# Counting edges with stretches of 6 end nodes and 256 edges in place of 8 and 384, in a graph network kernel on one core

## The chip, the cores and the metric

The kernel runs on one core of a Trainium2 chip. The metric is the device time of one execution in microseconds. A core has a matrix engine (TensorE, PE in the rows; PEld is its loading of weights), a vector engine (DVE), an activation engine (ACT), GpSimd (POOL) and a queue for transfers (SP). They run side by side and wait for each other by semaphores. [...]

## The reference

A graph has 2500 nodes with 256 features and 80000 edges, sorted by their end node `dst`. Three layers of an edge convolution follow a layer norm, and a last product takes the concatenation of all four node states.

```python
def _edge_conv(x, src, dst, W, b):
    xi = x[dst]
    xj = x[src]
    m = jnp.concatenate([xi, xj - xi], axis=-1) @ W + b
    s = jax.ops.segment_sum(m, dst, num_segments=N)
    cnt = jax.ops.segment_sum(jnp.ones((dst.shape[0],), m.dtype), dst, num_segments=N)
    return s / jnp.maximum(cnt, 1.0)[:, None]
...
for W, b in ((W0, b0), (W1, b1), (W2, b2)):
    h = jax.nn.relu(_edge_conv(h, src, dst, W, b))
    xs.append(h)
cat = jnp.concatenate(xs, axis=-1)
return cat @ Wf + bf          # h starts as max(layernorm(x), 0); x is added to this result
```

Since the sum over edges is linear, a layer needs only the matrix A of counts, A[s, d] being the number of edges from s to d. With Wt and Wb the two halves of W, the new state of node d is the ReLU of h[d] (Wt - Wb) + (sum over s of A[s, d] (h Wb)[s]) / count[d] + b.

## The kernel before

**Counting.** End nodes are cut into stretches of `W` = 8 consecutive nodes, `NW` = 313 of them. As edges are sorted by end node, the edges of a stretch lie in one run; for each stretch `CAP` = `CH` * 128 = 384 edges are taken from the run's start on, more than any stretch has. An edge has two keys: `key_m` is its start node within a tile of 128 nodes, `key_n` is (tile of the start node) * 8 + (end node within the stretch), and far outside for edges that are not of the stretch. `build(g, a)` makes the columns of A for a group of 384 end nodes. In each step it takes `BW` = 3 stretches and has DVE compare the keys with `iota_m` and `iota_n` (line 505): this gives 0/1 masks `one_m` (128 edges x 128 start nodes for each of 9 chunks of edges) and `one_n` (128 edges x 160 cells, `NB` = 20 tiles * 8). PE multiplies them (line 513), one product for each chunk, three accumulating for a stretch, and ACT copies 3 x 160 = 480 columns of counts from the PSUM bank into `a` (line 515). The masks lie in two buffers each (pool `hot`), so DVE can be two steps ahead of PE. A group has 16 such steps; `GT` = 3 tiles of 128 nodes make a group and 7 groups cover all nodes, the last with 200 columns.

**Preparation.** Where each stretch's run starts is found on the chip: `WG` blocks of 128 stretches (3 before) each gather one row of 625 end nodes (line 382, POOL), cast it (line 386, ACT) and count the entries below the stretch's first node (line 388, DVE). Then each block gathers its end and start nodes (line 404), forms the keys (lines 408 to 420), transposes them on PE (line 424) and stores them (line 426, ACT). `W` passes of DVE (line 430) count the edges of each end node. If the sum of these counts isn't the number of edges, another function (`general`) computes everything again.

**Layers.** `nodes_split` computes h Wb and splits it into two parts `zh`, `zl`. `layer(l, g)` runs `final` (line 525, the last product's share), `own` (line 541, h (Wt - Wb)) and 80 products of `zh` and `zl` with the counts (line 558). In layer 0 the counts of group g+1 are built while layer 0 runs on group g: `weave` interleaves the two in the program's text by a fixed ratio, 16 steps of `build` against 25 of `layer`. Each group of counts is also written to memory (line 520) and read back in layers 1 and 2 (line 607). A scheduler places the instructions of each engine in an order of its own from this text.

Of the kernel before, what the change touches and what calls it, by code (L numbers as in the profile page):

```python
# [9 lines left out]
I32 = mybir.dt.int32  # L10
# [259 lines left out]
def by_windows(ctx: ExitStack, tc: tile.TileContext, x, src, dst, Ws, bs, Wf, bf, out, missing):  # L270
    nc = tc.nc
    P = 128
    N, D = x.shape
    E = src.shape[0]
    NT = (N + P - 1) // P
    NP = NT * P
# [1 line left out]
    L = len(Ws)  # L278
    DC = D // P
    R = E // P  # L280
    W = 8
    CH = 3
    CAP = CH * P
    NW = (N + W - 1) // W
    NV = NW * W
    WG = (NW + P - 1) // P
    NB = NT * W
    BW = 3
    GT = 3
    G = GT * P  # L290
    GW = G // W
    NG = (NV + G - 1) // G
    FAR = 1024.0
    assert NP * FAR < 2 ** 24
    assert E == P * R and N % 2 == 0 and NV <= NP and BW * NB <= 512 and CAP < 4096 and NB <= 256
    assert E + P < 2 ** 24 and GW % BW == 0

    const = ctx.enter_context(tc.tile_pool(name="const", bufs=1))
# [6 lines left out]
    def bank():  # L305
        return ps.tile([P, 512], F32, name="bank")
# [5 lines left out]
    zl = const.tile([P, NT, D], F32R, name="zl")  # L312
    key_m = const.tile([P, NW, CH, 4], BF16, name="key_m")
    key_n = const.tile([P, NW, CH, 4], BF16, name="key_n")
    share = const.tile([P, NV], F32, name="share")
# [4 lines left out]
    iota_n = const.tile([P, NB], BF16, name="iota_n")  # L320
    b_sb = const.tile([P, L, DC], F32, name="b_sb")
    bf_sb = const.tile([P, D], F32, name="bf_sb")
    a_dram = [dram.tile([P, NT, G], F32, name=f"a_dram{g}") for g in range(NG)]
    deg_dram = dram.tile([2, WG * P * W], F32, name="deg_dram")


    pre = ctx.enter_context(ExitStack())
    pp = pre.enter_context(tc.tile_pool(name="pre", bufs=1))
# [26 lines left out]
    lim_i = pp.tile([P, WG], I32, name="lim_i")  # L355
    nc.gpsimd.iota(lim_i, pattern=[[P * W, WG]], base=0, channel_multiplier=W)
    lim = pp.tile([P, WG], F32, name="lim")
    nc.vector.tensor_copy(lim, lim_i)
    im_i = pp.tile([P, NB], I32, name="im_i")
    nc.gpsimd.iota(im_i, pattern=[[1, NB]], base=0, channel_multiplier=0)  # L360
    nc.vector.tensor_copy(iota_m, im_i[:, :P])
    nc.vector.tensor_copy(iota_n, im_i)

    first = pp.tile([P, 1], F32, name="first")
    nc.vector.tensor_copy(first, first_i)
# [11 lines left out]
    base = pp.tile([P, WG], F32, name="base")  # L377
# [21 lines left out]
    for i in range(WG):  # L399
# [21 lines left out]
        for keys, k in ((key_m, km), (key_n, kn)):  # L421
            pt = bank()
            for j in range(CH):
                nc.tensor.transpose(pt[:, j * P:(j + 1) * P], k[:, j * P:(j + 1) * P], ident)  # L424
            for j in range(CH):
                nc.scalar.copy(keys[:, i * P:i * P + n, j, :],
# [66 lines left out]
    def group_of(g):  # L493
        return g * G, min(G, NV - g * G)

    def build(g, a):
        w0, n = g * GW, group_of(g)[1] // W
        for s in range(0, n, BW):
            nb = min(BW, n - s)
            ws_ = slice(w0 + s, w0 + s + nb)  # L500
            one_m = hot.tile([P, BW * CH, P], BF16, name="one_m")
            one_n = hot.tile([P, BW * CH, NB], BF16, name="one_n")
            for one, iota, keys, m in ((one_m, iota_m, key_m, P), (one_n, iota_n, key_n, NB)):
# [110 lines left out]
def gnn_kernel(tc: tile.TileContext, x, src, dst, Ws, bs, Wf, bf, out):  # L614
    nc = tc.nc
    with tc.tile_pool(name="flag", bufs=1) as flag:
        missing = flag.tile([1, 1], I32, name="missing")
        by_windows(tc, x, src, dst, Ws, bs, Wf, bf, out, missing)
        again = nc.values_load(missing, min_val=0, max_val=1)
        with tc.If(again > 0):  # L620
            general(tc, x, src, dst, Ws, bs, Wf, bf, out)
# [28 lines left out]
```

## Time and profile before

| | |
|---|---|
| time of three runs | 614.01, 615.08 and 619.92 us, median 615.08 us |
| the profiled execution | 615.26 us, of which 613.5 us are its span from the first instruction to the last |
| busy in the span | PE 546.9, PEld 485.9, DVE 303.3, ACT 134.5, POOL 25.2 us |
[...]

A busy time counts the stretches in which an engine had at least one instruction under way. Products on PE overlap in the rows, since one begins before the one ahead has drained; the distance between two starts tells what one costs in a row of them, not its duration. In time the program has four parts: preparation to 48.5 us; `nodes_split` of layer 0 and the start of counting to 88 us; the counts of group 0 alone to 112 us; layer 0 interleaved with counting to 279 us. Then nothing is counted any more.

### The profile page before, as it was taken

The page shows a single profiled execution, that of the slowest core. Times are in us where ns is not written, and L with a number is a line of the kernel's source. Part 1 is how long each engine was busy: PE and PEld are TensorE (multiplying, and loading weights), DVE is VectorE, ACT ScalarE, POOL GpSimd, SP SyncE. Part 2 cuts the span into 40 slices and gives each one's busy share as a digit, 9 for nine tenths or more (in the row PEclk, how much of TensorE's full clock was granted, in tenths as well). Part 3 has the DMA queues.
Part 4 walks back from the last instruction along what each step waited for, and adds up shares of the span by engine and source line. Part 5 has one row for each costly group of instructions (what it writes and reads, how often), then busy time and mean ns, then how long its engine had stood idle before and what let it go on. Part 6 is the DMA issues. An engine that isn't in the chain of part 4 may idle for free.

```text
span 613.5 us, 8181 instructions
## 1 busy us (share of the span) xinstructions
PE 546.9 (89%) x3409; PEld 485.9 (79%) x3409; DVE 303.3 (49%) x617; ACT 134.5 (22%) x274; POOL 25.2 (4%) x37
## 2 busy tenths in 40 slices
PE   0036767999999999999999999999999999999996
PEld 0014555798989898989889999999988999999995
DVE  4694239989898989892240222202251220122233
ACT  0354643423333333331130000000031000000000
POOL 0422320000000000000000000000000000000000
PEclk9999997999999999999999999999999999999999
DMA  9314000606060605056920664344660533664013
GB/s 277 96 45 169 1 18 2 257 1 257 2 257 1 258 2 256 2 256 199 388 98 0 257 256 179 141 194 135 263 268 1 210 144 161 257 256 135 2 61 111
DMA packets 21277, 90.13 MB, mean 147 GB/s; under 512 B 2824, under 2 KB 18192, under 8 KB 18672
## 3 DMA queue, kind: packets, MB, share of 16 engines
q1 hardware_dynamic: 14272, 82.14, 34.1%
q10 hardware_dynamic: 6336, 5.26, 2.7%
q0 software_dynamic: 624, 2.14, 1.3%
q8 instruction: 28, 0.46, 0.3%
q14 instruction: 17, 0.14, 0.1%
HBM read 61.30 MB, written 28.23 MB: 146 GB/s over the span
## 4 chain that ended last, share of the span: by engine, by line
PE 83%; DVE 6%; DMA 4%; issue 3%; ACT 2%; POOL 1%; SPq 0%; DVEq 0%; POOLq 0%
PE pa L558 45%; PE bank L525 11%; PE bank L513 9%; PE bank L473 9%; PE bank L541 8%; DVE junk L430 2%; DMA wt<-in_L_gnn_W_dram 2%; DMA wb<-in_L_gnn_W_dram 1%; DVE one_n L505 1%; DVE one_m L505 1%; ACT zh L475 1%; ACT hT L485 1%; DMA es<-in_src_dram,start_i 1%; POOL rows L382 0%; DVE kn L418 0%
## 5 line engine op out<-in xcount | busy, mean ns | idle before, releaser
L558 PE MATMUL pa<-a,zh 128*128 128x384 f32 (+1 forms) x840 | 280.4, 341 | 0.7 <-ACT a L515 0.7
L558 PE MATMUL pa<-a,zl 128*128 128x384 f32 (+1 forms) x840 | 270.8, 329 | 0.0
L558 PEld LDWEIGHTS pa<-a,zh 128*128 128x128 f32 x840 | 158.4, 189 | 3.1 <-issue 0.9
L558 PEld LDWEIGHTS pa<-a,zl 128*128 128x128 f32 x840 | 158.5, 189 | 2.3
L563 DVE TENSOR_TENSOR v<-pa,share 128x384 f32<-128x384 f32 (+1 forms) x42 | 20.2, 523 | 213.0 <-PE pa L558 213.0
L505 DVE TENSOR_TENSOR one_n<-iota_n,key_n 128x1440 bf16<-128x1440 bf16 (+1 forms) x105 | 93.9, 895 | 0.0
L513 PE MATMUL bank<-one_n,one_m 128*128 128x160 bf16 x939 | 86.8, 240 | 6.5 <-DVE one_n L505 6.2
L513 PEld LDWEIGHTS <-one_m 128*128 128x128 bf16 x939 | 67.0, 101 | 25.4 <-issue 12.4
L505 DVE TENSOR_TENSOR one_m<-iota_m,key_m 128x1152 bf16<-128x1152 bf16 (+1 forms) x105 | 78.6, 749 | 11.8 <-PE bank L513 11.8
L515 ACT CAST a<-bank 128x480 fp32r<-128x480 f32 (+1 forms) x105 | 58.5, 558 | 110.4 <-PE bank L513 110.2
L543 ACT ACTIVATE u<-bank,b_sb 128x384 f32<-128x384 f32 (+1 forms) x42 | 23.5, 560 | 241.8 <-DVE acc L527 156.4
L525 PE MATMUL bank<-wf,hT 128*128 128x256 f32 x320 | 74.1, 381 | 0.0
L473 PE MATMUL bank<-wb,hT 128*128 128x256 f32 x240 | 60.0, 397 | 11.1 <-ACT hT L485 10.2
L525 PEld LDWEIGHTS bank<-wf,hT 128*128 128x128 f32 x320 | 59.5, 190 | 6.9
L473 PEld LDWEIGHTS bank<-wb,hT 128*128 128x128 f32 x240 | 44.7, 194 | 21.9 <-ACT hT L485 15.3
L541 PE MATMUL bank<-hT,wt 128*128 128x384 f32 (+1 forms) x168 | 55.2, 466 | 0.0
L476 DVE TENSOR_TENSOR zl<-bank,zh 128x256 fp32r<-128x256 f32 x60 | 25.2, 423 | 46.0 <-ACT zh L475 45.9
L541 PEld LDWEIGHTS bank<-hT,wt 128*128 128x128 f32 x168 | 30.7, 190 | 14.3
L475 ACT CAST zh<-bank 128x256 fp32r<-128x256 f32 x60 | 22.4, 373 | 61.1 <-PE bank L473 61.1
L527 DVE TENSOR_TENSOR acc<-acc,bank 128x256 f32<-128x256 f32 x80 | 30.4, 414 | 9.7 <-PE bank L525 9.7
L424 PE MATMUL bank<-ident,km 128*128 128x128 f32 x9 | 2.7, 439 | 33.1 <-ACT km L420 33.1
L424 PEld LDWEIGHTS bank<-ident,km 128*128 128x128 f32 x9 | 1.5, 212 | 34.2 <-ACT km L420 34.2
(66 smaller groups left out, 161.6 us busy)
## 6 DMA issues: line engine op xcount, KB each, us to landing
a<-a_dram SPq DMA_DIRECT2D x12, 3840.0 KB, 12.0
a_dram<-a SPq DMA_DIRECT2D x6, 3840.0 KB, 10.8
a<-a_dram SPq DMA_DIRECT2D x2, 2000.0 KB, 9.8
out_dram<-acc ACTq DMA_DIRECT2D x19, 128.0 KB, 1.7
a_dram<-a SPq DMA_DIRECT2D x1, 2000.0 KB
acc<-in_x_dram ACTq DMA_DIRECT2D x3, 640.0 KB, 8.0
some<-deg_dram SPq DMA_DIRECT2D x1, 1252.0 KB, 6.3
share<-deg_dram SPq DMA_DIRECT2D x1, 1252.0 KB
```

The costliest lines, as they stand in the source:

```text
L473: nc.tensor.matmul(pz[:, :D], hT[:, c, t * P:(t + 1) * P], ws[l][1][:, c, :], start=(c == 0), stop=(c == DC - 1))
L475: nc.scalar.copy(zh[:, t, :], pz[:, :D])
L476: nc.vector.tensor_sub(zl[:, t, :], pz[:, :D], zh[:, t, :].bitcast(F32))
L505: nc.vector.tensor_tensor(one[:, :k, :].rearrange("p k (m r) -> p k m r", r=4), iota.rearrange("p (m r) -> p m r", r=4).unsqueeze(1).to_br ...
L513: nc.tensor.matmul(pb[:, w * NB:(w + 1) * NB], one_m[:, w * CH + j, :], one_n[:, w * CH + j, :], start=(j == 0), stop=(j == CH - 1))
L515: nc.scalar.copy(a[:, :, s * W:(s + nb) * W].rearrange("p t (w c) -> p t w c", c=W), pb[:, :nb * NB].rearrange("p (w t c) -> p t w c", w=n ...
L525: nc.tensor.matmul(po[:, :D], hT[:, c, t * P:(t + 1) * P], wfs[l][:, c, :], start=(c == 0), stop=(c == DC - 1))
L527: nc.vector.tensor_add(acc[:, t, :], acc[:, t, :], po[:, :D])
L541: nc.tensor.matmul(pw_[:, :n], ws[l][0][:, c, o * P:(o + 1) * P], hT[:, c, c0:c0 + n], start=(c == 0), stop=(c == DC - 1))
L543: nc.scalar.activation(u[:, o, :n], pw_[:, :n], AF.Identity, bias=b_sb[:, l, o:o + 1])
L558: nc.tensor.matmul(pa[:, o, :n], z[:, k, o * P:(o + 1) * P], a[:, k, :n], start=(k == 0 and z is zh), stop=(k == NT - 1 and z is zl))
L563: nc.vector.tensor_mul(v[:, :n], pa[:, o, :n], share[:, c0:c0 + n])
```

## The change

Stretches have 6 end nodes (`W` = 6) and 256 edges (`CH` = 2), and a step of `build` takes `BW` = 4 of them. There are 417 stretches in place of 313, and `WG` is 4 in place of 3. The tile's place in `key_n` still counts in steps of 8 (`S`), so `iota_n` holds 20 x 6 = 120 of the values 0 to 159. A step has 8 products of 120 columns in place of 9 of 160; its masks are 8 x 128 and 8 x 120 elements on each partition in place of 9 x 128 and 9 x 160; ACT still copies 480 columns. A full group still has 16 steps. The last group has 198 columns in place of 200, and its build 33 stretches in place of 25, in 9 steps as before.

```diff
-    W = 8
-    CH = 3
+    W = 6
+    CH = 2
+    S = 8
     CAP = CH * P
     NW = (N + W - 1) // W
     NV = NW * W
     WG = (NW + P - 1) // P
     NB = NT * W
-    BW = 3
+    BW = 4
...
-    im_i = pp.tile([P, NB], I32, name="im_i")
-    nc.gpsimd.iota(im_i, pattern=[[1, NB]], base=0, channel_multiplier=0)
+    im_i = pp.tile([P, NT * S], I32, name="im_i")
+    nc.gpsimd.iota(im_i, pattern=[[1, NT * S]], base=0, channel_multiplier=0)
     nc.vector.tensor_copy(iota_m, im_i[:, :P])
-    nc.vector.tensor_copy(iota_n, im_i)
+    nc.vector.tensor_copy(iota_n.rearrange("p (t c) -> p t c", c=W),
+                          im_i.rearrange("p (t c) -> p t c", c=S)[:, :, :W])
```

In the interleaved part the order on PE stays the same but for the count of products in a burst and, twice in a group, one product of line 558 that changes sides of a burst. The order moves in the preparation. On ACT, at the casts of the gathered rows (`rows_f`), where the first two normalised tiles (`h0`) stand too; before:

```order
L461 ACTIVATE rs_385<-rs_385 128x20
L386 CAST rows_f_156<-rows_154 128x625
L480 ACTIVATE h0_398<-acc_76,off_389,rs_385 128x256
L480 ACTIVATE h0_410<-acc_76,off_389,rs_385 128x256
L420 CAST km_180<-lo_i_171 128x384
L426 CAST key_m_80<-bank_182 128x128x4 x3
L426 CAST key_n_81<-bank_189 128x128x4 x3
```

and now:

```order
L463 ACTIVATE rs_408<-rs_408 128x20
L388 CAST rows_f_158<-rows_156 128x625
L482 ACTIVATE h0_421<-acc_76,off_412,rs_408 128x256
L482 ACTIVATE h0_433<-acc_76,off_412,rs_408 128x256
L388 CAST rows_f_164<-rows_162 128x625
L422 CAST km_188<-lo_i_179 128x256
L428 CAST key_m_80<-bank_190 128x128x4 x2
L428 CAST key_n_81<-bank_195 128x128x4 x2
```

The cast of the fourth block's row stands behind the two `h0`. On POOL, at the gathers of the rows and of the edges (`ed`, `es`); before:

```order
L382 DMA rows_142<-in_dst_dram,blk_i_138 128x625
L382 DMA rows_148<-in_dst_dram,blk_i_138 128x625
L382 DMA rows_154<-in_dst_dram,blk_i_138 128x625
L404 DMA ed_166<-in_dst_dram,start_i_141 128x384
L404 DMA es_165<-in_src_dram,start_i_141 128x384
```

and now:

```order
L384 DMA rows_144<-in_dst_dram,blk_i_140 128x625
L384 DMA rows_150<-in_dst_dram,blk_i_140 128x625
L384 DMA rows_156<-in_dst_dram,blk_i_140 128x625
L384 DMA rows_162<-in_dst_dram,blk_i_140 128x625
L483 TENSOR_TENSOR acc_76<-acc_76,bf_sb_89 128x256 x2
L406 DMA ed_174<-in_dst_dram,start_i_143 128x256
L406 DMA es_173<-in_src_dram,start_i_143 128x256
```

Besides the fourth gather, two additions to `acc`, which stood behind all gathers, now stand ahead of those of the edges.

## Rows read from the trace of the kernel before

**Rows 1.** Page, chain that ended last: share of the span by line.
```profile
PE pa L558 45%; PE bank L525 11%; PE bank L513 9%; PE bank L473 9%; PE bank L541 8%; DVE junk L430 2%; DMA wt<-in_L_gnn_W_dram 2%; DMA wb<-in_L_gnn_W_dram 1%; DVE one_n L505 1%; DVE one_m L505 1%; ACT zh L475 1%; ACT hT L485 1%; DMA es<-in_src_dram,start_i 1%; POOL rows L382 0%; DVE kn L418 0%
```

**Rows 2.** Busy time by stage: stretch, length, engines' busy us, granted clock, transfers.
```profile
0.00:48.50 48.50, 6.15 (x21) 3.54 (x22) 34.30 (x141) 15.40 (x29) 11.65 (x19) 1.00 0.45 132
88.60:112.96 24.36, 17.19 (x153) 13.62 (x151) 24.07 (x33) 9.15 (x17) 0.00 (x0) 0.79 0.10 32
142.75:172.80 30.05, 30.05 (x245) 26.17 (x245) 28.08 (x42) 10.14 (x18) 0.00 (x0) 1.00 0.31 132
```

**Rows 3.** Groups of instructions, PE, one group of the interleaved part (142.75 to 172.80).
```profile
L513 PE MATMUL bank<-one_n,one_m 128*128 128x160 bf16 x144 | 12.7, 234 | 0.0
```

**Rows 4.** Timeline: products (PE), then weight loads (PEld), around one burst's end; start, duration.
```profile
151.66 0.44 PE L513 MATMUL bank<-one_n,one_m 128*128 128x160 bf16 x4
151.89 0.42 PE L558 MATMUL pa<-a,zh 128*128 128x384 f32 x1
152.15 0.33 PE L558 MATMUL pa<-a,zl 128*128 128x384 f32 x1
152.32 0.34 PE L558 MATMUL pa<-a,zh 128*128 128x384 f32 x1
...
151.30 0.18 PEld L513 LDWEIGHTS <-one_m 128*128 128x128 bf16 x3 [0.18 <-DVE one_n L505]
...
151.87 0.19 PEld L558 LDWEIGHTS pa<-a,zh 128*128 128x128 f32 x1
151.98 0.19 PEld L558 LDWEIGHTS pa<-a,zl 128*128 128x128 f32 x1
```

**Rows 5.** Timeline, PE: two of the 80 products of the last group, 200 columns.
```profile
292.05 0.28 PE L558 MATMUL pa<-a,zl 128*128 128x200 f32 x1
292.16 0.27 PE L558 MATMUL pa<-a,zh 128*128 128x200 f32 x1
```

**Rows 6.** Groups by shape, DVE, whole span: the masks at two widths, the counting passes.
```profile
L505 DVE TENSOR_TENSOR one_n<-iota_n,key_n 128x1440 bf16<-128x1440 bf16 x104 | 93.5, 899 | 0.0
L505 DVE TENSOR_TENSOR one_m<-iota_m,key_m 128x1152 bf16<-128x1152 bf16 x104 | 78.3, 753 | 11.8 <-PE bank L513 11.8
L430 DVE TENSOR_SCALAR_CACHE_REDUCE junk<-away 128x384 bf16<-128x384 f32 x16 | 7.9, 538 | 0.0
...
L371 DVE TENSOR_SCALAR_CACHE_REDUCE junk<-bank,lim 128x128 f32<-128x128 f32 x3 | 0.9, 343 | 0.0
...
L505 DVE TENSOR_TENSOR one_n<-iota_n,key_n 128x480 bf16<-128x480 bf16 x1 | 0.4, 400 | 0.0
L505 DVE TENSOR_TENSOR one_m<-iota_m,key_m 128x384 bf16<-128x384 bf16 x1 | 0.3, 349 | 0.0
```

**Rows 7.** Timeline, DVE: masks of group 0's third step and of the first step after it.
```profile
89.23 0.75 DVE L505 TENSOR_TENSOR one_m<-iota_m,key_m 128x1152 bf16<-128x1152 bf16 x1
...
110.28 0.75 DVE L505 TENSOR_TENSOR one_m<-iota_m,key_m 128x1152 bf16<-128x1152 bf16 x1
```

**Rows 8.** Timeline of the preparation: ACT, DVE and POOL, starts of the blocks.
```profile
23.69 0.70 ACT L386 CAST rows_f<-rows 128x625 f32<-128x625 int32 x1
24.42 0.87 DVE L388 TENSOR_SCALAR_CACHE_REDUCE junk<-rows_f,lim 128x625 bf16<-128x625 f32 x1 [0.33 <-ACT rows_f L386]
25.42 1.09 ACT L480 ACTIVATE h<-acc,off,rs 128x256 f32<-128x256 f32 x2 [1.03 <-DVE off L464]
29.12 0.47 DVE L408 TENSOR_SCALAR away<-ed,lim 128x384 f32<-128x384 int32 x1 [3.42 <-DMA ed<-in_dst_dram,start_i]
33.73 1.41 POOL L481 TENSOR_TENSOR acc<-acc,bf_sb 128x256 f32<-128x256 f32 x2
35.64 0.41 DVE L408 TENSOR_SCALAR away<-ed,lim 128x384 f32<-128x384 int32 x1
47.36 0.74 DVE L505 TENSOR_TENSOR one_m<-iota_m,key_m 128x1152 bf16<-128x1152 bf16 x1
```

**Rows 9.** Busy time by stage, as in rows 2: a stretch within group 0's counting.
```profile
102.48:109.31 6.83, 5.90 (x39) 4.63 (x40) 6.83 (x10) 2.45 (x5) 0.00 (x0) 0.51 0.00 0
```

More of the change, by code (lines that the diff above doesn't have):

```diff
@@ L293, in by_windows @@
     FAR = 1024.0
-    assert NP * FAR < 2 ** 24
-    assert E == P * R and N % 2 == 0 and NV <= NP and BW * NB <= 512 and CAP < 4096 and NB <= 256
+    assert NP * FAR < 2 ** 24 and W <= S and NT * S <= 256
+    assert E == P * R and N % 2 == 0 and NV <= NP and BW * NB <= 512 and CAP < 4096
     assert E + P < 2 ** 24 and GW % BW == 0
```

## The prediction

> **What bounds the kernel now.** I read the chain that ended last first, then the busy times by stage, then single rows. In the chain the reader is to see that PE carries it, with 9% of the span in the products that count edges, line 513 [rows 1]. The stages tell where those lie on the path [rows 2]. In the interleaved part PE is busy all of its 30.05 us in each group, while DVE has 28.08 and ACT 10.14: PE is the bound there, with DVE close behind. While group 0 is counted alone (88.60 to 112.96) it is the other way round: DVE is busy 24.07 of 24.36 us and PE 17.19. In the preparation DVE has the most, 34.30 of 48.50 us, but in a chain with gathers. From 279 us on nothing is counted, so more than half of the time has no part in it: layers 1 and 2 and the last product are the same but for a last group of 198 columns instead of 200.
>
> **The products in the interleaved part.** Four products of a burst take 0.44 us from the first start to the last end [rows 4], and one lasts 0.234 us [rows 3], so starts stand (0.44 - 0.234)/3 = 0.069 us apart. [...] For 120 columns I take 50 + 2.5 = 52.5 ns.
>
> What ends a burst matters too. The product of line 558 behind it starts its weight load at 151.87, when the last narrow product starts; the second such load follows 0.11 us later, at 151.98, and the second product begins at 152.15, 0.26 us behind the first, where 0.17 is usual (from there to the next start, 152.32) [rows 4]. The wide load of 0.11 us thus covers the last narrow product, whether that takes 69 or 52 ns. So a burst counts by its gaps: eight of 69.2 ns before, 554 ns, seven of 52.5 now, 368 ns, and 186 ns are saved. Five groups are built fully in this part with 16 bursts each, the last group's build has 8 full bursts and one of two products instead of three: 88 x 0.186 + 0.09 = **16.5 us saved**. If the last product counted fully it would be 88 x 0.203, 1.5 us more.
>
> Does the weight load let a product be that short? It is loaded anew for each product, 128 columns. Three bf16 loads are through in 0.18 us, the drain of the last counted in [rows 4]: at most 0.06 us each. With that bound as the pace, 88 x 7 x 7.5 ns = 4.6 us of the gain are lost. I take none, because the end of the third load is drain that would overlap, and keep 4.6 for the range. [...]
>
> [...]
>
> DVE must keep up. Its masks have a slope: one_m (753 - 349)/768 = 0.526 ns per element, one_n (899 - 400)/960 = 0.520 [rows 6]. A step has 128 and 480 elements fewer: 67 + 250 = 317 ns less. DVE's 28.08 us of a group become 28.08 - 16 x 0.317 = 23.0, against PE's 30.05 - 16 x 0.186 = 27.1. PE stays the bound, with more room than before. ACT copies 480 columns in 16 steps as before, with runs of 6 cells in place of 8; its 10.14 of 30 us hide even a doubling.
>
> **Group 0 alone.** Two steps are masked ahead; the third starts at 89.23 and the seventeenth, the first of group 1, at 110.28: 14 steps of 1.504 us, DVE without a gap [rows 7]. They lose 14 x 0.317 = 4.4 us. The last burst behind them is 0.2 us shorter: **4.6 us saved**. PE does not take over, even at half clock: in the stretch at 0.51 DVE is still busy all of 6.83 us [rows 9], and eight products of 100 ns fit into 1.19 us better than nine of 133 into 1.50.
>
> The clock is what may be given back here. PE's level fell and rose while group 0 was counted; one low stretch of 6.83 us ended at 109.31, just ahead of the dense work [rows 9]. A shorter step moves this boundary. If a low stretch like that falls wholly on the start of layer 0, where PE is the bound, it costs 3.4 us; if the luck stays, nothing. The stage's mean clock of 0.79 [rows 2] says that some 4 in 10 of it ran at the lower level; caught in the middle, such a stretch costs 1.7 us, and four tenths of that are **0.6 us lost**.
>
> **Preparation.** A fourth block comes in. Its gather of rows is on POOL's queue behind the other three, and I take it to have landed when ACT gets to it. Its cast stands on ACT behind the two h0: 1.09 us, then the cast 0.70, then DVE's count 0.87 [rows 8], one more pass of line 371 of about 0.3, and some 0.15 for handing over, before the starts are known and the edge gathers may go: 3.1 us later. On POOL the two additions that now stand ahead of the edge gathers wait for the same h0; they take 1.41 us [rows 8] and are done while ACT casts and DVE counts, 1.6 us of cover. If that cover were gone, the gathers would go up to 1.4 us later.
>
> Against that the blocks get shorter. The first begins at 29.12, the second at 35.64, and the masks follow the third at 47.36 [rows 8]: 18.24 us, 5.86 for a block and 0.66 of waiting in the first. A block has 12 DVE instructions in place of 14 (6 counting passes, not 8), 256 wide. If all of their time went with width, it would be 5.86 x 12/14 x 2/3 = 3.35 us; by the passes, 343 ns at 128 and 538 at 384 [rows 6], 440 at 256, it would be 5.86 x 12/14 x 0.82 = 4.1. I take 3.7: 4 x 3.7 + 0.7 = 15.5, which is 2.8 us less, 1.2 to 4.2 by the two ends. Net **0.3 us lost**, from 1.1 won to 1.9 lost; with the POOL cover gone 3.3 lost.
>
> **Costs at nothing.** The key transposes and casts become 8 of each kind per key in place of 9, beside DVE's blocks. The last group's two columns less, and its rows of 792 bytes in memory, are hidden: in layers 1 and 2 the read of a group is issued while the group ahead of it is at work. nodes_split waits on ACT and PE, not on what changes.
>
> **The sum.** From the profiled execution: 615.26 - 16.5 - 4.6 + 0.6 + 0.3 = **595.1 us** (its span 613.5 becomes 593.3). It stands 0.2 us from the median of the runs, 615.08, so I leave it there.
>
> **The rivals.** *The pair of load and product does not get faster than today's 69 ns*, since something other than columns sets it. Then seven gaps of 69.2 in place of eight save 88 x 0.069 = 6.1 us: 615.26 - 6.2 - 4.6 + 0.9 = 605.4 us. [...]
>
> *The pair has a higher floor of its own, and more products make the kernel slower or the same.* 834 products need not be cheaper than 939. The nearest price is the pair with fp32 weights, 0.11 us [rows 5]: 88 x (7 x 111 - 554) ns = 19.6 us lost, 631 us in all. It decides from a pace of about 86 ns on; from 76 to 96 ns the result lies within 1%, about what a measurement of this kernel can tell from no change. Against it: pairs of 160 columns already run at 69 ns.
>
> [...]
>
> *The masks lose their rate.* one_n has rows of 120 instead of 160. If that cost its 0.52 ns per element twice over, it would take 0.15 + 960 x 1.04 = 1.15 us, and a step 0.18 more than now, with one_m's saving: 2.6 us lost in group 0, and DVE with 28.08 + 16 x 0.18 = 31 us would bound each group, 1 us over today's: 623 us in all. Nothing in the rows speaks for it; the inner runs stay at four elements.
>
> *The change doesn't count all edges*, and the other function runs: in the reference's inputs the fullest stretch of 6 nodes has 241 edges, under 256, so this gets no chance.
>
> **How the numbers follow.** The forecast 0.86; the floor at 69 ns 0.06; a floor between, within 1%, 0.04; a floor above that, or slow masks, 0.04. Faster by over 1%: 0.86 + 0.06 = 0.92; within 1%: 0.04; slower: 0.04. The range goes from 595.1 - 1.5 (burst ends) - 1.4 (preparation) - 0.6 (clock) = 591.6 down to 591, and up by a load of 60 ns (4.6) with part of clock (2.8) and preparation (1.6 to 3.0), which will hardly come together: 602. The floor at 69 ns stays outside.
>
> **What would show it.** In the profile after, products of line 515 should stand 52 ns apart and a full group of layer 0 take 27.1 us with PE busy throughout; DVE's steps in group 0 should be 1.19 us; blocks should start some 3.7 us apart from about 32 us on, and masks begin near 47.7; from the end of layer 0 on, every distance should be as before. I would be wrong if PE waits for masks in layer 0, if gaps stay near 69 ns, if a low clock reaches into layer 0, or if the preparation ends microseconds later.

## The result, and the profile after

The change makes the kernel faster: 595.75 us median of four runs (595.69 to 598.03) against 616.79 us for four of the kernel before, a ratio of 0.967 (95% interval 0.961 to 0.973). The forecast was 595.1 us, the range 591 to 602. The profiled execution took 595.69 us with a span of 593.4 us from the first instruction to the last, against 615.26 and 613.5.

I take the stages in the order of the prediction. The busy times by stage come first: the stretch and its length, then busy microseconds of PE, PEld, DVE, ACT and POOL, the granted clock as a share of full speed, share and rate of the transfers.

```profile
0.00:47.80 47.80, 6.24 (x20) 2.87 (x20) 32.16 (x151) 15.39 (x29) 13.97 (x22) 1.00 0.46 138
87.80:108.15 20.35, 15.13 (x136) 11.64 (x134) 19.15 (x33) 9.13 (x17) 0.00 (x0) 0.59 0.11 38
91.56:112.04 20.48, 17.14 (x119) 13.07 (x120) 17.65 (x31) 7.82 (x14) 0.00 (x0) 0.50 0.23 98
137.01:164.09 27.08, 27.08 (x230) 23.21 (x229) 23.28 (x42) 10.03 (x18) 0.00 (x0) 1.00 0.35 147
```

The last row answers to the group of 30.05 us [rows 2]: the group is 2.97 us shorter, PE is busy throughout, and DVE has 23.28 us where 23.0 were worked out. The second row shows group 0 at a mean clock of 0.59 in place of 0.79, and the third is the reason: one stretch of 20.48 us at the lower level, a granted clock of 0.50, which ends at 112.04. The first wide product of layer 0 stands at 106.67, so 5.4 us of that stretch lie in layer 0.

The page's chain that ended last, by line, shows the narrow products (now line 515) at 7% where they had 9% [rows 1]:

```profile
PE pa L560 48%; PE bank L527 12%; PE bank L475 10%; PE bank L543 9%; PE bank L515 7%; DMA wb<-in_L_gnn_W_dram 1%; DVE junk L432 1%; ACT zh L477 1%; DVE one_m L507 1%; DVE one_n L507 1%; ACT hT L487 1%; DMA rows<-in_dst_dram,blk_i 1%; DMA es<-in_src_dram,start_i 0%; ACT rows_f L388 0%; DVE junk L390 0%
```

The next rows are of the kernel after: the narrow products as a group of one stretch (137.01 to 164.09), then a burst in the timeline, products (PE) and weight loads (PEld) behind it.

```profile
L515 PE MATMUL bank<-one_n,one_m 128*128 128x120 bf16 x129 | 9.7, 217 | 0.0
...
144.94 0.59 PE L515 MATMUL bank<-one_n,one_m 128*128 128x120 bf16 x8
145.34 0.42 PE L560 MATMUL pa<-a,zh 128*128 128x384 f32 x1
145.61 0.34 PE L560 MATMUL pa<-a,zl 128*128 128x384 f32 x1
...
145.32 0.19 PEld L560 LDWEIGHTS pa<-a,zh 128*128 128x128 f32 x1
145.43 0.19 PEld L560 LDWEIGHTS pa<-a,zl 128*128 128x128 f32 x1
```

Eight products last 0.59 us, one 0.217: starts stand (0.59 - 0.217)/7 = 0.053 us apart. The end of a burst is what it was [rows 4]: the first wide load starts with the last narrow product, the second 0.11 us later, and the second wide product 0.27 us behind the first.

DVE's masks by shape, and the third and the seventeenth step of group 0 in its timeline (answering to [rows 6] and [rows 7]):

```profile
L507 DVE TENSOR_TENSOR one_m<-iota_m,key_m 128x1024 bf16<-128x1024 bf16 x104 | 71.5, 687 | 22.4 <-PE bank L515 22.4
L507 DVE TENSOR_TENSOR one_n<-iota_n,key_n 128x960 bf16<-128x960 bf16 x104 | 67.5, 649 | 0.0
...
88.46 0.68 DVE L507 TENSOR_TENSOR one_m<-iota_m,key_m 128x1024 bf16<-128x1024 bf16 x1
...
104.85 0.68 DVE L507 TENSOR_TENSOR one_m<-iota_m,key_m 128x1024 bf16<-128x1024 bf16 x1
```

Fourteen steps take 16.39 us, 1.171 each. In the timeline of the preparation (ACT, POOL, DVE) the reader sees the fourth cast behind the two `h0`, POOL's two additions done before the edge gathers can go, and the blocks:

```profile
25.55 1.09 ACT L482 ACTIVATE h<-acc,off,rs 128x256 f32<-128x256 f32 x2 [1.03 <-DVE off L466]
26.23 1.40 POOL L483 TENSOR_TENSOR acc<-acc,bf_sb 128x256 f32<-128x256 f32 x2 [4.44 <-ACT h L482]
26.55 0.70 ACT L388 CAST rows_f<-rows 128x625 f32<-128x625 int32 x1
27.28 0.87 DVE L390 TENSOR_SCALAR_CACHE_REDUCE junk<-rows_f,lim 128x625 bf16<-128x625 f32 x1 [1.76 <-ACT rows_f L388]
28.82 0.96 POOL L406 DMA_INDIRECT ed<-in_dst_dram,start_i  x1 [1.19 <-DVE start_i L394]
31.66 0.35 DVE L410 TENSOR_SCALAR away<-ed,lim 128x256 f32<-128x256 int32 x1 [3.10 <-DMA ed<-in_dst_dram,start_i]
35.97 0.35 DVE L410 TENSOR_SCALAR away<-ed,lim 128x256 f32<-128x256 int32 x1
46.70 0.68 DVE L507 TENSOR_TENSOR one_m<-iota_m,key_m 128x1024 bf16<-128x1024 bf16 x1
```

The first block starts at 31.66 (29.12 before), the masks at 46.70 (47.36 before): the four blocks win back more than the fourth gather costs. From the second block on they are 3.58 us apart, (46.70 - 35.97)/3.

The start of layer 0 is where the clock shows, in the timeline of PE, kernel after:

```profile
106.67 0.66 PE L560 MATMUL pa<-a,zh 128*128 128x384 f32 x1 [0.69 <-issue]
107.13 1.02 PE L515 MATMUL bank<-one_n,one_m 128*128 128x120 bf16 x8
107.94 3.73 PE L527 MATMUL bank<-wf,hT 128*128 128x256 f32 x8
...
112.17 1.09 PE L527 MATMUL bank<-wf,hT 128*128 128x256 f32 x4
```

Eight products of line 527 take 3.73 us at the lower level, 0.43 us from start to start at a granted 0.50; the next four take 1.09 at the higher, 0.22 us apart at 1.00. The second wide product of layer 0 follows, and in the kernel before the first and the second:

```profile
116.55 0.42 PE L560 MATMUL pa<-a,zl 128*128 128x384 f32 x1
```

```profile
111.91 0.41 PE L558 MATMUL pa<-a,zh 128*128 128x384 f32 x1 [0.69 <-ACT a L515]
...
119.92 0.42 PE L558 MATMUL pa<-a,zl 128*128 128x384 f32 x1
```

One more difference lies in a part that the prediction took as unchanged. Successive groups of 80 wide products in layer 1, in the chain of waits (start, duration); first the kernel before, then after:

```profile
361.63 14.08 PE pa L558 x80
380.88 14.08 PE pa L558 x80
```

```profile
304.17 14.14 PE pa L560 x80
...
323.48 13.87 PE pa L560 x80
...
342.52 14.13 PE pa L560 x80
```

Before, all twelve full groups of layers 1 and 2 take 14.07 or 14.08 us. After, they take 14.13 and 13.87 by turns, which is 6 x 0.21 - 6 x 0.05 = 1.0 us less in sum. That part of the code isn't touched; but the smaller keys move the two count buffers `a` by 1728 bytes on each partition, from 157216 and 187936 to 155488 and 186208 in the built programs.

**Where the 20 us came from**, by the two spans' own times. The third mask step comes 0.77 us earlier (0.66 of it in the preparation). Fourteen steps of group 0 are 4.66 us shorter. Layer 0 is 13.7 us shorter from its first wide product (111.91 before, 106.67 after) to the first product of layer 1's transforms in a row (303.89 and 284.92). Layers 1 and 2 give 1.0. From the seventeenth mask step to the first wide product it takes 0.2 us longer than before (1.82 and 1.63). The sum is 20.0, against 20.1 between the spans. In layer 0 the 13.7 us hide a loss: from the first wide product to the second, with four bursts between them, it took 8.01 us before (111.91 to 119.92) and should take 8.01 - 4 x 0.186 = 7.27; it takes 9.88 (106.67 to 116.55). With the last burst of group 0, which should have got 0.2 shorter and got 0.2 longer, the low clock costs 3.0 us.

### The profile page after: what moved, and what is told of

It is laid out like the page before. It is cut to its first block, busy times and chain, and to the rows that moved or that the text cites. A ratio compares the mean times of both kernels' runs of the same rounds, so it can differ in the third digit from the quotient of the medians.

```text
span 593.4 us, 7989 instructions
## 1 busy us (share of the span) xinstructions
PE 529.2 (89%) x3302; PEld 467.1 (79%) x3302; DVE 269.3 (45%) x627; ACT 133.6 (23%) x274; POOL 27.0 (5%) x40
## 4 chain that ended last, share of the span: by engine, by line
PE 85%; DVE 6%; ACT 3%; DMA 3%; issue 2%; SPq 0%; POOL 0%; DVEq 0%
PE pa L560 48%; PE bank L527 12%; PE bank L475 10%; PE bank L543 9%; PE bank L515 7%; DMA wb<-in_L_gnn_W_dram 1%; DVE junk L432 1%; ACT zh L477 1%; DVE one_m L507 1%; DVE one_n L507 1%; ACT hT L487 1%; DMA rows<-in_dst_dram,blk_i 1%; DMA es<-in_src_dram,start_i 0%; ACT rows_f L388 0%; DVE junk L390 0%
## 5 line engine op out<-in xcount | busy, mean ns | idle before, releaser
L507 DVE TENSOR_TENSOR one_m<-iota_m,key_m 128x1024 bf16<-128x1024 bf16 (+1 forms) x105 | 71.8, 684 | 22.7 <-PE bank L515 22.7
L527 PE MATMUL bank<-wf,hT 128*128 128x256 f32 x320 | 76.1, 388 | 0.0
L515 PE MATMUL bank<-one_n,one_m 128*128 128x120 bf16 x834 | 67.1, 229 | 4.5 <-DVE one_n L507 3.9
L515 PEld LDWEIGHTS <-one_m 128*128 128x128 bf16 x834 | 50.4, 104 | 23.5 <-DVE one_n L507 10.7
L507 DVE TENSOR_TENSOR one_n<-iota_n,key_n 128x960 bf16<-128x960 bf16 (+1 forms) x105 | 67.8, 645 | 0.0
L527 PEld LDWEIGHTS bank<-wf,hT 128*128 128x128 f32 x320 | 60.7, 194 | 7.3
```

The lines of the kernel that those rows point to most:

```text
L507: nc.vector.tensor_tensor(one[:, :k, :].rearrange("p k (m r) -> p k m r", r=4), iota.rearrange("p (m r) -> p m r", r=4).unsqueeze(1).to_br ...
L515: nc.tensor.matmul(pb[:, w * NB:(w + 1) * NB], one_m[:, w * CH + j, :], one_n[:, w * CH + j, :], start=(j == 0), stop=(j == CH - 1))
L527: nc.tensor.matmul(po[:, :D], hT[:, c, t * P:(t + 1) * P], wfs[l][:, c, :], start=(c == 0), stop=(c == DC - 1))
```

## The experiments

The theory from here: PE's narrow products were the bound in the interleaved part and DVE's masks in group 0; what the prediction had too small is the loss by the clock at the start of layer 0, and what it had at nothing is the place of the count buffers. The first four runs took one of these each; every one is the kernel after with the edit shown (`...` marks lines left out). The single times of runs without repetition are one execution each.

**Masks as large as before, products as now.** More keys are compared than the products use. The products stay as they are, but the scheduler also moves some of them, as told below.

```
-            one_m = hot.tile([P, BW * CH, P], BF16, name="one_m")
-            one_n = hot.tile([P, BW * CH, NB], BF16, name="one_n")
-            for one, iota, keys, m in ((one_m, iota_m, key_m, P), (one_n, iota_n, key_n, NB)):
-                k = nb * CH
+            one_m = hot.tile([P, 9, P], BF16, name="one_m")
+            one_n = hot.tile([P, 12, NB], BF16, name="one_n")
+            for one, iota, keys, m, full in ((one_m, iota_m, key_m, P, 9), (one_n, iota_n, key_n, NB, 12)):
+                k = full if nb == BW and w0 + s + 6 <= NW else nb * CH
...
```

> The changed kernel with DVE's work undone: a step writes masks as large as before the change (9 x 128 and 1440 elements, the added ones are read by nobody), while its products stay 8 of 120 columns. By the theory (DVE sets the steps of group 0 alone, PE sets the interleaved part) a step of group 0 goes from 1.17 back to about 1.50 us, 4.7 us in all; in the interleaved part DVE's load per group of about 23 us grows by 16 x 0.33 to some 28.3 us, over PE's 27.08, so a group takes 28.3 to 28.6 us: 607 us in all. Rival, that masks hide behind PE there as they did before: groups stay at 27.1 us and the sum is 600.4.

Measured: 605.37 us. The fourth group of the interleaved part in the busy times by stage:

```profile
200.53:228.92 28.39, 27.44 (x233) 23.43 (x229) 27.83 (x42) 9.81 (x18) 0.00 (x0) 1.00 0.33 140
```

DVE is busy 27.83 of 28.39 us and PE no longer throughout (27.44): DVE has become the bound here, with steps 1.49 us apart. The products still stand 53 ns apart. In the first two groups PE stays full all the same, since its order has moved: the stretch from 147.86 to 176.54 holds 89 wide products where a group has 80, and from the third group on 17 or 19 wide products stand in one row, where the kernel after has at most 8 between two bursts. The smaller masks, with the order that comes with them, are thus worth 9.7 us of the change by these two executions: 14 x 0.333 = 4.7 in group 0 and 4.0 in layer 0, which takes 193.1 us from its first product of line 527 to layer 1's (189.2 after); the other 1.0 lies ahead of these. How much of the 4.0 is the order's isn't separated. By this run, products cut without their masks would have won little more than half. In group 0 the clock's low stretch is 23.9 us long here (bursts of 0.98 us in place of 0.58, the first of them at 92.39 with 0.82).

**More products, same masks.** Three products of each step are done twice, so a burst has 11.

```
+                if w < 3:
+                    nc.tensor.matmul(pb[:, w * NB:(w + 1) * NB], one_m[:, w * CH, :], one_n[:, w * CH, :],
+                                     start=True, stop=True)
```

> The changed kernel with three products more in each burst of eight (the first product of three stretches is issued twice), masks as in the change. By the theory each added product costs 52.5 ns of PE in the interleaved part: 16 x 3 x 0.0525 = 2.5 us for each full group, 29.6 us instead of 27.08, 13.9 us in all, less up to 2.4 us if the busier PE gets its clock back before layer 0: 607 to 609.6 us. Rival, that the gain of the interleaved part came from lighter masks and not from PE: groups stay near 27.1 us and the time under 600.

Measured: 608.88 us, and in the busy times by stage:

```profile
145.41:174.90 29.49, 29.49 (x279) 25.64 (x278) 23.77 (x42) 10.14 (x19) 0.00 (x0) 1.00 0.32 135
```

A group is 2.41 us longer than after, 48 products at 50 ns. PE is the bound, and a product costs its distance to the next, as the sum took it. The clock stays full here: its mean over the span is 0.999, 0.980 in the kernel after.

**The same three, in group 0 alone.** The condition becomes `w < 3 and g == 0`.

> The changed kernel with three products more in each burst of group 0 alone. There DVE sets the pace, so at full clock nothing should be lost; at the low level a burst of eleven takes some 1.27 us and a step of group 0 with it, 0.1 us more. Theory, that a PE with little to do in group 0 is left at the low clock, which then reaches into layer 0 and costs some 2.4 us there: the clock is back before layer 0 starts, its first group takes 27.1 us instead of 28.9, 593 to 595 us. Rival, that the low stretch has nothing to do with how much PE does there: the stretch stays some 20 us long and the time rises to about 597 us.

Measured: 593.89 us. Group 0's steps, then the second interleaved group, in the busy times by stage; then PE's timeline at the start of layer 0, where the first row is the same work as the 3.73 us above:

```profile
90.89:107.28 16.39, 10.11 (x151) 7.99 (x147) 16.39 (x30) 7.93 (x15) 0.00 (x0) 1.00 0.06 17
109.74:136.82 27.08, 27.08 (x230) 23.34 (x229) 21.14 (x37) 9.90 (x19) 0.00 (x0) 1.00 0.36 151
...
109.01 1.95 PE L530 MATMUL bank<-wf,hT 128*128 128x256 f32 x8
111.22 1.09 PE L530 MATMUL bank<-wf,hT 128*128 128x256 f32 x4
```

Group 0's fourteen steps take 16.39 us as after, so the extra products are free there, DVE being the bound; and the clock stays at its higher level through it, 1.00 where the kernel after has 0.59 (87.80 to 108.15). From the seventeenth mask step (107.28) to the second group's first product of the last matrix (136.06) it takes 28.78 us, and 32.00 after (104.85 to 136.85): by this pair the clock's loss is **3.2 us**, by the rows above 3.0. The whole came down by 1.8 only, in single executions: another 1.1 us are won in a wait at the head of layer 1, and 2.4 are lost again ahead of group 0 (its third step stands at 90.89, not 88.46), which the next run made plain.

**The count buffers put back** to where they were before the change, with 1728 unused bytes.

```
+    gap = ctx.enter_context(tc.tile_pool(name="gap", bufs=1))
+    hole = gap.tile([P, 432], F32, name="hole")
+    nc.vector.memset(hole[:, 0:1], 0.0)
     apool = ctx.enter_context(tc.tile_pool(name="apool", bufs=2))
```

> The changed kernel with 1728 unused bytes on each partition ahead of the two count buffers, so that these lie at the addresses that they had before the change. In the changed kernel the wide products of layers 1 and 2 stand 176.7 and 173.3 ns apart in turn, buffer by buffer; before they stood 176.05 apart in both. Theory, that the place of the buffer in memory sets this: 176 ns in both again, 12 groups of layers 1 and 2 together about 1 us longer, 596 to 597 us. Rival, that something else of the change does: the alternation stays and the time with it, 595.7.

Measured: 602.03 us, 5 us over the expectation. The chain of waits has the wide groups at 14.08 us again, as expected, and shows where the rest is: one row for each tile of nodes_split, 2.07 us in the first tiles and 1.15 later.

```profile
61.76 2.08 PE bank L475 x4
64.72 1.59 PE bank L475 x4
67.03 1.15 PE bank L475 x4
...
347.78 14.08 PE pa L563 x80
```

The granted clock reads 1.00 in this stretch throughout; that the first tiles run at the lower clock is read from their pace. In the kernel after, products of 256 columns stand 0.43 us apart in the first two tiles, as those of line 527 do at a granted 0.50, and 0.22 us in the tiles behind, as at 1.00. Read so, five tiles and a part of the sixth run at the lower clock here; in the kernel after it was two. A tile takes 2.97 us there and 1.87 at the full clock. From the masks' first step to the third it is 45.64 us here and 41.76 after, 3.9 us more; the preparation ended 0.9 later, the wide products of layers 1 and 2 cost 1.0, and layer 0 takes 0.4 more: 6.2 of the 6.3 us. So, by this reading, what raised this time is no work of the kernel but the moment at which the clock comes up in nodes_split, and it differs from one execution to another. This is the table of the profiles in which group 0 stands behind nodes_split and the masks follow after four blocks, with the kernel before:

| kernel | tiles at the lower clock | first to third mask step, us |
|---|---|---|
| products in the preparation (below) | none | 39.40 |
| buffers moved by 32 bytes (below) | 1 and a part | 41.40 |
| after | 2 | 41.76 |
| before | 2 | 41.87 |
| masks as large as before | 2 | 41.96 |
| more products in group 0 | 3 and a part | 43.35 |
| after, once more (below) | 3 and a part | 43.56 |
| more products | 4 and a part | 44.59 |
| both additions (below) | 4 and a part | 44.83 |
| buffers put back | 5 and a part | 45.64 |

**The place moved by 32 bytes only** (a hole of 8 elements in place of 432).

> 32 unused bytes on each partition ahead of the two buffers of counts. Moving them by 1728 bytes gave the wide products their old 176.05 ns in both buffers in place of 173.3 and 176.7. Theory: the pace hangs on where the moving operand lies, in steps finer than a kilobyte: 32 bytes change it too, in one buffer at least (anything from 173 to 177 ns). Rival: only the distance from other tiles or a coarser place counts, and 32 bytes leave 173.3 and 176.7 as they are. The time as a whole: 595 to 602 us, since the tiles of nodes_split at the lower clock differ from run to run; so only the pace is read.

Measured: 594.38 us, and every full group of layers 1 and 2 takes 13.88 or 13.89 us: 173.5 ns for a wide product, in both buffers. 32 bytes are enough. I come back to this below.

**Narrower stretches**, to see where the weight load stops the products.

```
-    W = 6
-    CH = 2
+    W = 2
+    CH = 1
...
-    BW = 4
+    BW = 8
```

> Stretches of 2 nodes with 128 edges, one product of 40 columns for each, 8 in a step, 24 steps in a group, 1250 products, 10 blocks in the preparation. Read is the distance of products in a burst. Theory of the prediction: columns set the pace of 52.5 ns at 120, 50 by columns and 2.5 fixed, so 40 columns go below it, to 22 ns by the same sum or to where the weight load stops them, 30 to 45 ns. Rival: the load of 128 weights takes 50 ns already, so that the change has met its floor by chance: 50 to 53 ns. DVE has 24 steps of about 1.0 us in a group and the rest of its work, 28 us, and bounds the groups of layer 0 either way; with six more blocks in the preparation, 2.3 us each, and 6 us more in group 0 the time is 615 to 630 us.

Measured: 614.78 us, just under the expected range. The timeline of PE has a burst:

```profile
171.12 0.37 PE L515 MATMUL bank<-one_n,one_m 128*128 128x40 bf16 x8
171.33 0.42 PE L560 MATMUL pa<-a,zl 128*128 128x384 f32 x1
```

The products stand 25 ns apart (median of 620 distances), each with its own load of 128 bf16 weights, so 53 ns at 120 columns are not a floor. But 25 is more than the prediction's sum gives: of its 50 + 2.5 ns for 120 columns, a third of the 50 is 16.7, and with the 2.5 that makes 19.2 (the 22 of the expectation is a slip). From 160 columns to 120 the distance fell by 16 ns, 0.40 a column, and from 120 to 40 by 28, 0.35 a column. What sets the 25 no run shows. A group takes 26.66 us, less than after although it has 24 bursts: I had DVE at 28 us a group and it is busy 24.8. The rival of a floor at 76 ns or more falls here.

**Group 0 counted beside nodes_split.** The statistics and `h0` get small pools of their own, and the steps of group 0 are written between the tiles.

```
-    for t in range(NT):
-        h0 = pw.tile([P, D], F32, name="h0")
+    def normal(t):
+        h0 = mid2.tile([P, D], F32, name="h0")
...
-    run(build(0, tiles[0]))
+    weave(build(0, tiles[0]), GW // BW, normals(), NT)
```

> The counts of group 0 are written into the program between the tiles of nodes_split of layer 0 (16 steps against 20 tiles) and no longer behind them, with small pools of their own for what both need. Theory: in nodes_split DVE is idle for more than 7 tenths of the time (8 to 10 of 39 us busy), a tile takes 1.87 us because the normalised tile goes from ACT over PE to ACT, PE, ACT and DVE, and the masks of a step (1.17 us) fit beside it; what stood alone, some 18 us from 88.5 to 106.7, shrinks to under 5, a tile of nodes_split takes up to 2.3 us, and the time is 583 to 588 us. With PE at work on both from the start, the low stretch of the clock that reaches into layer 0 should go too. Rival: the chain of ACT and PE in nodes_split is stretched by as much as the masks and the copies of counts take from it, since ACT then has 1.87 us of work per tile as well; then the time stays at 594 to 598 us.

Measured: 584.47 us median of four runs (583.48 to 591.33), ratio to before 0.950 (0.944 to 0.956). From the second mask step to the first wide product, in the busy times by stage; first this kernel, then after:

```profile
48.75:96.83 48.08, 34.60 (x245) 25.74 (x245) 27.04 (x54) 30.28 (x73) 13.41 (x18) 1.00 0.16 55
```

```profile
48.34:106.67 58.33, 42.91 (x249) 30.99 (x247) 27.86 (x56) 30.94 (x74) 13.07 (x18) 0.87 0.16 50
```

10.25 us are won here, and 1.6 at the start of layer 0, where the clock is full now (the mean of the span is 0.997). The rival has a part of it: a tile with a step beside it takes 2.47 us, 0.6 more, which is ACT's copy of counts (0.56 us), now in the chain of ACT and PE.

**Products in the preparation**, 16 behind each block's transposes, whose results nobody reads.

```
+        pd = bank()
+        for j in range(16):
+            nc.tensor.matmul(pd[:, :NB], iota_m, iota_n, start=True, stop=True)
```

> Alone 16 products of iota_m and iota_n behind the key transposes of each of the four blocks of the preparation, 64 in all, written to a bank that nobody reads. Theory: the first tiles of nodes_split run at the lower clock, 2.97 us each in place of 1.87, and their number differs from run to run (about two and a half in the changed kernel's profile, three and a half and five and a half in two of the experiments), which is where most of the spread between runs comes from; with PE at work ahead of them the clock rises earlier. With no tile at the lower clock: 593 to 594 us and a narrower spread; the preparation is not longer, since the products take 1.6 us of a block of 3.6 on an engine that waits. Rival: the clock doesn't rise for so little, or falls again before the tiles: 595 to 602 us as without them. Second rival: the products hold up the transposes of the next block, and the preparation ends 1 to 3 us later.

Measured: 592.81 us median of four runs (591.63 to 594.04), ratio to before 0.961 (0.958 to 0.963). In its profile the pace is the faster one before the first tile (the last block's 16 products take 1.00 us, those of the block ahead 1.81), all twenty run at 1.13 us a row, and the preparation isn't longer (masks from 46.59). The low stretch in group 0 is there all the same, 17.07 us long (bursts of 0.98 us in place of 0.58 from 90.81 on).

**Both additions**: these products and the three of group 0.

> warm, and in group 0 three more products in each step, as in busy_start. Theory: two losses stand apart. The tiles of nodes_split at the lower clock go by the products in the preparation, and the low stretch that reaches into layer 0, 2.4 us by the rows of the changed kernel against 0.6 in the prediction, goes by the products in group 0: 590.0 to 591 us, that is 1.8 to 2.4 us under warm's 592.8, and the runs lie within 1 us of each other. Rival: the lower clock in layer 0 comes from something else than the sparse products ahead of it, and returns a few microseconds later: 592 to 594 us as warm.

Measured: 591.58 us median of five runs (590.32 to 596.26). The clock is full through group 0 (the mean of the span is 0.998) and the first group of layer 0 takes 27.06 us, as expected. But the profiled run is the one of 596.26 us, and its chain has four tiles and a part at the lower clock in spite of the products ahead of them:

```profile
49.31 2.07 PE bank L478 x4
...
58.20 2.07 PE bank L478 x4
61.16 1.57 PE bank L478 x4
63.45 1.15 PE bank L478 x4
```

So 16 products a block don't make sure of the clock. Three profiles have them: by the pace it is up ahead of the first tile in two (the last block's 16 products take 1.00 us, from 45.98 in the run above and from 46.45 with all of it together, below), and in this one it comes within the row at 61.16, those 16 products taking 1.81; without them it comes up after the first tile has begun in every profile. That they shift the odds is likely but not shown by so few. The runs didn't lie within 1 us; the four others have 590.32 to 592.42.

**The kernel after once more**, on the same chip as the run before.

> The changed kernel once more, on the same chip as the other two. Theory: the time differs by the count of the first tiles of nodes_split at the lower clock, 1.1 us for each over the two and a half of its first profile: 595 to 600 us, and the profile's own time follows its count of such tiles. Rival: what differs between runs lies elsewhere, in the transfers of the preparation, and the tiles are the same in all runs.

Measured: 598.41 us median of four runs (594.80 to 599.97), ratio to before 0.970 (0.966 to 0.974). Its profile, at 597.23 us, has three tiles and a part at the lower clock, and the masks' third step comes 1.42 us later than in the first profile; the time is 1.54 longer. So the same program takes this stretch differently from one execution to the next. The theory holds for the profiled pair; the runs without a profile are not shown to differ for this reason.

**All of it together**: group 0 beside nodes_split, the products in the preparation, and 64 unused bytes, so that the buffers lie at multiples of 128 bytes like those moved by 32.

> The version that the runs so far point to: group 0 counted between the tiles of nodes_split, 64 products in the preparation as in warm, and 64 unused bytes ahead of the buffers of counts, which puts them at a multiple of 128 bytes as 32 bytes did in shift_32. Theory: early_counts took 583.5 to 585.3 us in three runs of four and 591.3 in one; the clock at full from the first tile on takes 1 to 2 us and the slow run out, and wide products at 173.5 ns in all groups of layers 1 and 2 in place of 173.3 and 176.7 by turns another 80 x 12 x 1.5 ns = 1.4 us: 580 to 583 us. Rival: the products of the preparation are of no use here, since early_counts has PE busier in nodes_split anyway, and the place works otherwise with the other tiles in memory: 583 to 586 us.

Measured: 585.65 us median of six runs (584.79 to 588.57), over the expectation and not better than counting beside nodes_split alone. The chain has

```profile
310.84 14.13 PE pa L573 x80
```

in all twelve full groups, the worst pace so far: 12 x 14.13 against 6 x 13.87 + 6 x 14.13 is 1.6 us more, and the profiled spans differ by 1.0 (582.7 and 581.7). The place is the reason by these two profiles, and a multiple of 128 bytes is not it. The clock, up ahead of the first tile here, won next to nothing: the first wide product starts at 96.70, without the products in the preparation at 96.83.

**The place 4096 bytes above the good one.** Group 0 beside nodes_split, no products in the preparation, a hole of 1728 bytes.

> early_counts with 1728 unused bytes ahead of the buffers of counts: they lie 4096 bytes above those of shift_32, where all groups of layers 1 and 2 ran at 173.5 ns. Theory: the place within 4096 bytes sets the pace, so all twelve full groups run at 173.5 ns in place of 173.3 and 176.6 by turns, 1.4 us less than early_counts' 583.5 to 585.3 us: 582 to 584 us. Rival: the pace doesn't follow the place in this way, as the 176.7 ns of all groups in together suggest (its buffers lay at a multiple of 128 bytes too); then any of the paces seen so far, 583 to 586 us.

Measured: 582.36 us median of six runs (581.59 to 584.20), ratio to before 0.945 (0.942 to 0.947); 2 us under the version without the hole, though on another chip. In the chain all twelve groups are at the good pace:

```profile
310.75 13.88 PE pa L570 x80
329.81 13.88 PE pa L570 x80
```

This is the fastest version tried. The paces by place of the two buffers, one full group of layers 1 and 2:

| place on the partition, bytes | full groups, us |
|---|---|
| 157216, 187936 (before; buffers put back) | 14.08 |
| 155488, 186208 (after, and five others) | 13.87 and 14.13 by turns |
| 155520, 186240 (moved by 32) | 13.88 |
| 157888, 188608 (counts beside nodes_split) | 13.87 and 14.13 by turns |
| 161984, 192704 (narrower stretches) | 13.87 and 14.13 by turns |
| 157952, 188672 (together) | 14.13 |
| 159616, 190336 (the last) | 13.88 |

The same places gave the same paces in every kernel, but for the first full group of layer 1, which took 13.97 us in three profiles with the buffers at 155488 and 186208. Both pairs of places that lie 4096 bytes apart agree. By what rule a place is good stays open. Where two paces take turns, they don't belong to the buffers. A layer has seven groups and there are two buffers, so a group's buffer in layer 2 is the other one than in layer 1; yet the slower pace comes first in both layers of the kernel after. And the same program, run once more, has the other order in layer 2. The first two full groups there, first profile and then the second:

```profile
448.46 14.13 PE pa L560 x80
467.76 13.87 PE pa L560 x80
```

```profile
449.77 13.87 PE pa L560 x80
468.81 14.13 PE pa L560 x80
```

So the place goes with which paces occur, and what gives a group one of the two is not found.

## Why the prediction was right

**The pace.** 52.5 ns were forecast, 53 came. Products with a load each go down to 25 ns at 40 columns, so neither the load nor a floor sets the 53. No run shows the 50 and the 2.5 of which the 52.5 was made; what the runs show is 69 ns at 160 columns, 53 at 120 and 25 at 40 (19.2 by that sum), and at a granted 0.50 133 ns at 160 (before) and 100 at 120 (after). Nor does one show the 69.2: its row gives 68.7 and the trace 69; at 68.7 a burst saves 182 ns in place of 186, 0.4 us in all. The full group is 2.97 us shorter, against 16 x 0.186 = 2.98. That a burst counts by its gaps because the wide load covers its last product is borne out by the burst's rows. The load of at most 0.06 us, kept as an end of the range, was a cautious bound.

**DVE.** 23.28 us a group against 23.0; without the smaller masks DVE would have been the bound from the third group on, as the first experiment shows, with the order on PE that comes with it. In group 0 the steps lost 14 x 0.333 = 4.66 us against 4.4, and with the last burst 4.6 were forecast: the last burst, 0.2 of it, was lost to the low clock.

**The preparation.** Forecast 0.3 lost, measured 0.66 won, within the bounds given. The fourth gather costs 2.5 us (31.66 against 29.12) where 3.1 were taken, and the four blocks 15.0 where 15.5 were. POOL's two additions ended at 27.63, 1.2 us ahead of the gather of edges: the cover was there.

**The clock is the term that was mis-sized:** 0.6 us forecast, 3.0 measured. The step that failed is "caught in the middle, such a stretch costs 1.7 us, and four tenths of that are 0.6" (four tenths of 1.7 are 0.7, a slip of 0.1). It took the low stretch to stay 6.83 us long, and only its place to be a matter of luck. With 8 products in a step of 1.17 us the engine stayed at the lower level for 20.48 us in one piece, until the dense work of layer 0; with 9 of 160 columns in a step of 1.50 it had come up twice. With 11 in a step of 1.17 it never fell in group 0, in three profiles (mean clock of the span 0.997 to 0.999); with the same 8 and group 0 alone it fell in all five, for 20.48 us in four (0.980 or 0.981) and 17.07 in one (0.985). The mean clock of 0.79 was read as a chance of place, where in these profiles the long low stretch came with the count of products in a step, though its length still differed by 3.4 us between executions.

**What the prediction had at nothing** in layers 1 and 2 was 1.0 us won, by the place of buffers that the change moves without naming them. Taken together, 2.4 us too little for the clock stand against 1.1 from the preparation up to the third step, 1.0 from the place and 0.3 from the steps: the sum came out within 0.7 us of the median (and the span, 593.3 forecast, within 0.1) because these cancel. That closeness is luck; the saving of the products, the largest term, was right in itself.

**The rivals.** A floor at 69 ns, one above 86, and slower masks are all excluded by rows (53 ns, and masks of 687 and 649 ns where the slopes gave 686 and 649). The spread between executions, 595 to 600 us for the changed kernel over eight runs, is wider than the forecast's own terms of preparation and clock had; the two profiles of it differ by the tiles of nodes_split at the lower clock, a cause that the prediction didn't look at, though the two slow tiles were there before the change as well.

## What to carry to other kernels

A short product in bf16 went from 69 ns at 160 columns to 53 at 120 here, and at 40 it took 25, still less than half; so cutting unused columns from a TensorE-bound stage paid in full, the engine which prepares the operands being cut along with it. Ask of every shorter stage ahead of dense work whether TensorE still has enough in it to keep its clock: here three useless products in a step, where it waited anyway, went with a clock of 1.00 in place of 0.59 and cost that stage no time (16.39 us with them and without), where the low clock carried into the stage where it is the bound had cost 3.2 us. And when one stage has its engine idle behind a chain, weaving the next stage's work into it was worth more here (11 us) than any other change tried on top.

## What was not expected of the hardware

- Wide products (384 columns, fp32 weights) stand 173.3 to 176.7 ns apart; which paces occur goes with where the moving operand lies on the partition, and 32 bytes change it. Over layers 1 and 2 the ends lie 3.0 us apart (12 x 0.25).
- In eight profiles of kernels that do the same up to there or nearly so, the products of nodes_split went over to the faster pace, read as the higher clock, at the earliest within the row at 52.49 us (moved by 32 bytes) and at the latest within the row at 64.72 (buffers put back); each tile at the slower pace costs 1.1 us.
- A product of 40 columns with its own load of 128 bf16 weights followed the one ahead by 25 ns (narrower stretches).
